# Position-bias rows in two column halves, and two small transposes moved from TensorE to VectorE, in a windowed-attention and expert layer

## The chip, the cores and the metric

The kernel runs on one core of one Trainium2 chip. The metric is the device time in microseconds of one execution; the time given for a kernel is the median of several. TensorE is the matrix engine (PE in the profile; PEld are its weight loads), VectorE is DVE, ScalarE is ACT, GpSimd is POOL, and SyncE (SP) only issues transfers. All data are float32.

## The reference, cut to what matters

The input x is (2, 128, 256, 256): batch, channels, rows, columns. One layer: layer norm over the channels, attention in windows of 8 x 8 pixels with keys from 12 x 12 pixels around them, an output projection and a residual; then, per pixel, a second norm, a router that picks 2 of 8 experts, and their weighted sum as a second residual.

```python
qkv = jnp.einsum('bchw,oc->bohw', x, W_qkv)          # 4 heads of 32
attn = jnp.einsum('bnd,bmd->bnm', q * SCALE, k)
attn = attn + rel_pos_emb(q, rel_height, rel_width) + FIXED_MASK
out = jnp.einsum('bnm,bmd->bnd', jax.nn.softmax(attn, axis=-1), v)
x = x + jnp.einsum('bchw,oc->bohw', out, W_out)
...
router_probs = jax.nn.softmax(t @ router_w + router_b, axis=-1)
top_p, top_i = jax.lax.top_k(router_probs, 2)
```

The mask leaves only keys whose row offset and column offset from the query are both even, so pixels attend only to pixels of their own row parity and column parity. The bias of a query and a key is a product of the query with a row of rel_height (chosen by their difference in rows) plus one with a row of rel_width (difference in columns). After the mask, a window has, for each parity, 4 x 4 queries and 6 x 6 keys, with nine differences in each direction.

## The kernel before, in words

**Tiling.** The image is cut into 64 strips of 8 rows (32 per batch element). A strip has four planes, one per row and column parity, so there are 256 planes of 4 rows x 128 columns = 512 pixels, 32 windows of 16. The channels lie on the 128 partitions. The main loop runs over planes, `n` from 0 to 256 + 6; the last seven rounds only finish experts. Inside `manual_schedule` the order of the instructions on TensorE, VectorE, ScalarE, GpSimd and SP is the order of the calls in the loop.

**One round of the loop**, in the order of TensorE's queue, with the lines of the profile:

- `scores(n)`: the bias is added into the score banks by small matmuls of 32 x 64 array tiles (L447, operand `au`), then queries times keys (L464, `qs`, `kcol`). ScalarE takes the exponential (L472).
- first part of `project(n+1)`: half of the values, `pvv` (L368), copied by ScalarE (L375).
- second part: `pu` (L383), the product of the normed plane `xn` with `wrel`. `wrel` has 128 columns, of which each head uses 18: nine differences of height and nine of width. VectorE turns it in 32 x 32 blocks into `uT` (L385). The call of `states[n + 1]["shift"]()` right after copies from `uT`, with a stride that makes the difference depend on the query's place, into `auT` (L348, two copies), and turns that back into `au` (L353), which the next round's scores read.
- third and fourth part: keys `pk` (L395) and queries `pq` (L417), copied by ScalarE (L406, L413, L419).
- `spread`: the gates `g` (40 columns, four tiles of 128 pixels times 8 experts, a mean and the next layer norm's factor) are turned by TensorE into `pg` (L622), copied by ScalarE to `gT` (L624), stored by SP to `gd` in DRAM (L626), and read back to all partitions: `rb` (L630), `sb` (L659) and `gb` for each expert (L654). 
- four expert products `acc` (L679) of an older row.
- `attend(n)`: row sums (L485), then weights times values (L495); VectorE turns, inverts and multiplies (L505 to L515).
- `norms`: ScalarE squares the rows (L541), TensorE sums them, and makes the router's logits, in 128 x 32 array tiles, `plt` (L547). ScalarE copies them to `lT` (L555), TensorE turns that into `plg` (L558), and VectorE makes mean and deviation from it (`rstd`, L227 to L234, with two ScalarE steps). `route` in the next round (L582 to L615) makes the gates.
- the other half of the values (L368), one product, plg, two products, `out_project` `po` (L523), one product.

VectorE also multiplies the tokens with the gates (`xe`, L670, six of eight experts; GpSimd does two), and adds po and acc to x (L528, L685). GpSimd makes `xn` (L271) and the key columns `xcol` (L330).

**What sets the order.** Every engine works through its own queue in order, and an instruction that waits holds up those behind it. The buffers in PSUM (`ps_mm`) are three, shared by pvv, pu, pk, pq, pg, plt, plg and po. Each DMA in the built program uses one of eight completion semaphores in turn and waits until the DMA before it on that semaphore has landed; before, SP issues all DMAs of the loop. `addr_align` at the head of a round (L786) pads TensorE's program so that each round starts at the same place of a block of 256 instructions.

The softmax here doesn't subtract the row's maximum and nothing guards it: scores larger than these inputs give would overflow.

## Time and profile before

| | us |
|---|---|
| time, median of 3 runs (4543.13 to 4551.57) | 4548.22 |
| the profiled execution: its own time | 4549.69 |
| its span, first to last instruction | 4547.9 |
| TensorE busy | 4490.6 |
| VectorE busy | 3826.1 |
| ScalarE busy | 1582.6 |
| GpSimd busy | 1321.7 |

The profile is one execution. The view of groups gives for each line and engine the number of instructions, their summed time, the mean of one, and how long the engine stood idle just before them and for whom. The chain of waits is followed back from the last instruction: at each step to what released it. Of the span 97% lies on TensorE in that chain. A float32 matmul appears as two MATMUL passes, each with a weight load. Their single durations (595 ns for 512 columns) overlap with the next pass; the chain gives what each adds to the path (430 ns). Groups that the change concerns:

| line | engine, tile | count | mean ns |
|---|---|---|---|
| L383 | PE pu | 512 | 596 |
| L385 | DVE uT | 256 | 717 |
| L348 | DVE auT, 96 elements | 512 | 208 |
| L353 | DVE au | 256 | 1051 |
| L555 | ACT lT | 260 | 266 |
| L558 | PE plg | 260 | 273 |
| L622 | PE pg | 260 | 271 |
| L624 | ACT gT | 260 | 259 |
| L626 | SP gd, 20 KB | 245 | - |

### The profile page before, as it was taken

Reading aid. Unit: us, or ns where it says so; the run is one execution under the profiler, and the core shown is the slowest. Engines: PE = TensorE matmul, PEld = TensorE weight load, DVE = VectorE, ACT = ScalarE, POOL = GpSimd, SP = SyncE. Lnnn points to the kernel's source line nnn. Section 1 sums busy time; section 2 is a strip of 40 time slices with the busy share of each in tenths; the row PEclk is TensorE's granted clock in tenths of the full one; section 3 lists DMA queues with packets and bytes.
Section 4 is the critical chain, followed back from the end, with each engine's and each line's share of the span. In section 5 each row is a group of like instructions: output and inputs, shape, how many; then the busy total and the mean of one; then the engine's idle time right before and its main releaser. Section 6 shows DMA issues by size and latency. Waiting matters only on the chain.

```text
span 4547.9 us, 224166 instructions
## 1 busy us (share of the span) xinstructions
PE 4490.6 (99%) x96841; PEld 2708.2 (60%) x96841; DVE 3826.1 (84%) x11330; ACT 1582.6 (35%) x4542; POOL 1321.7 (29%) x1812
## 2 busy tenths in 40 slices
PE   7999999999999999999999999999999999999997
PEld 5665666565666666666666666666666656656653
DVE  5888888888888888888888888888888888888886
ACT  3333333333333333333333333333333333333331
POOL 1232323232323223232323232323232323232221
PEclk9999999999999999999999999999999999999999
DMA  2565666566556666665656665656666656666655
GB/s 76 176 191 180 190 179 191 181 190 180 189 180 189 183 186 184 186 185 183 188 181 186 183 188 181 190 180 190 180 190 180 191 179 190 182 187 181 188 163 181
DMA packets 457786, 824.84 MB, mean 181 GB/s; under 512 B 52480, under 2 KB 64356, under 8 KB 456804
## 3 DMA queue, kind: packets, MB, share of 16 engines
q1 hardware_dynamic: 456074, 810.21, 59.0%
q8 instruction: 769, 12.60, 1.1%
q14 instruction: 213, 1.74, 0.1%
q10 hardware_dynamic: 730, 0.29, 0.0%
HBM read 737.95 MB, written 72.34 MB: 178 GB/s over the span
## 4 chain that ended last, share of the span: by engine, by line
PE 97%; DVE 1%; issue 1%; DMA 0%; ACT 0%; POOL 0%; SPq 0%; ACTq 0%; DVEq 0%; POOLq 0%
PE acc L679 38%; PE pvv L368 12%; PE att L464 7%; PE att L495 6%; PE plt L547 6%; PE pu L383 5%; PE po L523 5%; PE pk L395 5%; PE pq L417 5%; PE att L447 3%; PE att L485 3%; PE pg L622 1%; PE plg L558 1%; DMA gb<-gd 0%; DVE xe L670 0%
## 5 line engine op out<-in xcount | busy, mean ns | idle before, releaser
L679 PE MATMUL acc<-xe,ew 128*128 128x512 f32 x4096 | 1921.7, 595 | 6.5 <-DVE xt L685 2.6
L679 PEld LDWEIGHTS acc<-xe,ew 128*128 128x128 f32 x4096 | 720.8, 191 | 788.1 <-issue 780.3
L670 DVE TENSOR_TENSOR xe<-xs,gb 128x512 f32<-128x512 f32 x1536 | 950.5, 686 | 10.9 <-DMA gb<-gd 2.2
L674 POOL COPY last<-xe 128x1 f32<-128x1 f32 x256 | 48.3, 189 | 3110.8 <-DVE gb L653 3103.7
L670 POOL TENSOR_TENSOR xe<-xs,gb 128x512 f32<-128x512 f32 x512 | 652.3, 1275 | 5.7 <-PE att L495 2.7
L368 PE MATMUL pvv<-wt,xcol 128*128 128x128 f32 x4096 | 595.1, 288 | 4.2 <-POOL xcol L330 3.1
L368 PEld LDWEIGHTS pvv<-wt,xcol 128*128 128x128 f32 x4096 | 497.2, 191 | 66.6 <-issue 51.9
L555 ACT COPY lT<-plt 128x128 f32<-128x128 f32 x260 | 69.3, 266 | 1141.3 <-PE plt L547 1141.3
L271 POOL TENSOR_TENSOR xn<-xt,rb 128x512 f32<-128x512 f32 x249 | 375.9, 1510 | 79.9 <-DMA rb<-gd 68.1
L464 PE MATMUL att<-qs,kcol 32*64 32x32 f32 x32768 | 391.7, 226 | 2.4 <-issue 2.4
L464 PEld LDWEIGHTS att<-qs,kcol 32*64 32x64 f32 x32768 | 390.3, 130 | 2.6 <-issue 2.6
L375 ACT COPY vv<-pvv 128x512 f32<-128x512 f32 x512 | 300.3, 586 | 207.4 <-PE pvv L368 191.4
L495 PEld LDWEIGHTS att<-pT,vv 64*32 64x32 f32 x32768 | 347.8, 105 | 36.7
L472 ACT ACTIVATE pT<-att 128x1024 f32<-128x1024 f32 x256 | 262.1, 1024 | 253.7 <-PE att L464 250.3
L495 PE MATMUL att<-pT,vv 64*32 64x32 f32 x32768 | 342.5, 200 | 0.0
L385 DVE STREAM_TRANSPOSE uT<-pu 128x512 f32<-128x512 f32 x256 | 183.5, 717 | 150.2 <-PE pu L383 150.2
L541 ACT ACTIVATE sq<-xt 128x512 f32<-128x512 f32 x505 | 292.1, 628 | 0.0
L353 DVE STREAM_TRANSPOSE au<-auT 128x512 f32<-128x512 f32 x256 | 269.2, 1051 | 9.0
L406 ACT COPY kcol<-pk 128x560 f32<-128x560 f32 (+2 forms) x344 | 174.3, 507 | 268.5 <-PE pk L395 265.7
L523 PE MATMUL po<-o,wt 128*128 128x512 f32 x512 | 261.8, 593 | 4.1 <-DVE r__0_619 L227 1.0
L383 PE MATMUL pu<-xn,wrel 128*128 128x512 f32 x512 | 263.6, 596 | 0.0
L417 PE MATMUL pq<-xn,wt 128*128 128x512 f32 x512 | 262.2, 593 | 0.5 <-issue 0.2
(2700 smaller groups left out, 5579.8 us busy)
## 6 DMA issues: line engine op xcount, KB each, us to landing
gb<-gd SPq DMA_DIRECT2D x2048, 256.0 KB
xt<-in_x_dram SPq DMA_DIRECT2D x256, 256.0 KB
sb<-gd SPq DMA_DIRECT2D x256, 256.0 KB
out_dram<-xt SPq DMA_DIRECT2D x256, 256.0 KB
rb<-gd SPq DMA_DIRECT2D x249, 256.0 KB
gd<-gT SPq DMA_DIRECT2D x245, 20.0 KB
ew<-in_L_ffn_expert_w_dram SPq DMA_DIRECT2D x1, 512.0 KB
eb<-in_L_ffn_expert_b_dram SPq DMA_DIRECT2D x1, 512.0 KB
```

What stands on the lines that cost most here:

```text
L271: eng.tensor_tensor(xn[i % 2][:, :, :, k, 1 : PC + 1], ln1_src(i, k).rearrange("p (y j x) -> p y x j", y=2, x=2), rb.rearrange("p (y j x) ...
L368: nc.tensor.matmul(pv[:, t * P : (t + 1) * P], lhsT=xl[:, t0 + t].rearrange("p a k -> p (a k)"), rhs=wv, start=True, stop=True,)
L375: nc.scalar.copy(vv[:, t0 : t0 + 4, :].rearrange("p t c -> p (t c)"), pv)
L383: nc.tensor.matmul(pu, lhsT=wrel, rhs=inner, start=True, stop=True)
L417: nc.tensor.matmul(pq, lhsT=wq, rhs=inner, start=True, stop=True)
L464: nc.tensor.matmul(sc[rows, h, 32 * t : 32 * t + 32], lhsT=kk[hp, half * HP + t, :], rhs=qs[hp, m0 : m0 + 2].rearrange("p m a s -> p (m a ...
L495: nc.tensor.matmul(av[hp, half, 32 * t : 32 * t + 32], lhsT=vv[rows, t, hp], rhs=pT[rows, h, 32 * t : 32 * t + 32], start=True, stop=True,)
L523: nc.tensor.matmul(po, lhsT=wo, rhs=state["o"].rearrange("p f z -> p (f z)"), start=True, stop=True)
L541: nc.scalar.activation(sq, src, AF.Square)
L547: nc.tensor.matmul(plt[32 * t : 32 * t + 32, :P], lhsT=rw[:, j], rhs=src[:, t * P : (t + 1) * P], start=(j == srcs[0][0]), stop=(j == srcs ...
L670: eng.tensor_tensor(self.xe[e], self.xs, self.gb.pop(e), ALU.mult)
L679: nc.tensor.matmul(self.acc, lhsT=ew[:, e, :], rhs=self.xe.pop(e), start=(e == 0), stop=not self.xe)
```

## The change

**Bias.** One of the nine differences of each direction is subtracted from the other eight when `relbd` is built, which adds the same number to all scores of a query and so leaves the softmax as it is. A head then has 16 columns instead of 18, and `wrel` has 64. `pu` becomes two matmuls: the first two rows of the plane into PSUM partitions 0 to 63, the other two into 64 to 127, each 256 columns. `uT` has 256 columns. `shift` makes four copies (two of 96 elements on 64 partitions each, two of 48 on all), two memsets for the difference that is now zero, and a transpose of 256 columns into `both`. A new function `send`, called after the squares of `norms`, moves `both` with eight DMAs on ScalarE's queue, each 16 partitions x 1 KB, to `au`, which is now two fixed buffers that TensorE reads in runs of 8 numbers.

**Statistics and gates.** The copy `lT` goes; VectorE turns `plt` from PSUM straight into `plg` in PSUM in 32 x 32 blocks. `g` is one of three fixed buffers of 2 x 4 x 8 columns; VectorE turns it in SBUF into `gT`, and SP stores it with two DMAs in runs of 128 B. TensorE's `pg` and ScalarE's copy go. `spread` is called before `pu` instead of after `pq`.

```diff
-    relbd = ctile([P, P], "relbd")
+    relbd = ctile([P, HEADS * NB], "relbd")
...
     def shift(uT, n, state):
 
-        for j in range(2):
-            shifted = uT[:, :, :, NU * j + 3 : NU * j + 9]
-            dims = [list(d) for d in shifted.ap]
-            dims[1 + j][0] -= 1
+        to = auT[n % 2]
+        for up, (rows, start) in enumerate(((slice(0, 64), 3), (slice(64, P), 1))):
+            src = uT[rows, :, :, start : start + 6]
+            step, block = src.ap[1][0], src.ap[2][0]
+            dims = [list(src.ap[0]), [step - 1, 2], [block // 2, 8], [1, 6]]
             nc.vector.tensor_copy(
-                auT[n % 2][:, :, :, 6 * j : 6 * j + 6],
-                bass.AP(shifted.tensor, shifted.offset, dims),
+                to[rows, :, :, :, 0:6].rearrange("p a s h k -> p a (s h) k"),
+                bass.AP(src.tensor, src.offset, dims),
             )
-        au = work.tile([P, 2 * NP, PR, 4], F32, tag="au", name=f"au{n}")
-        nc.vector.transpose(au.rearrange("p m a s -> p a s m"), auT[n % 2])
-        state["au"] = au
+        src = uT[:, :, :, NU + 2 : NU + 8]
+        step, block = src.ap[1][0], src.ap[2][0]
+        for h in range(2):
+            dims = [list(src.ap[0]), [step, 2], [block - 1, 4], [1, 6]]
+            nc.vector.tensor_copy(
+                to[:, :, :, h, 6:12], bass.AP(src.tensor, src.offset + h * NB, dims)
+            )
+
+        nc.vector.memset(to[0:64, 0, :, :, 5:6], 0.0)
+        nc.vector.memset(to[:, :, 0, :, 11:12], 0.0)
+        both = work.tile([P, 2 * NP, 8], F32, tag="both", name=f"both{n}")
+        nc.vector.transpose(
+            both.rearrange("p m (a s) -> p a s m", a=2), to.rearrange("p a s h k -> p a s (h k)")
+        )
+        state["both"] = both
+
+    def send(n, state):
+
+        both = state.pop("both")
+        for up in range(2):
+            for h in range(HEADS):
+                r = (up * HEADS + h) * NB
+                nc.scalar.dma_start(au[n % 2][h * DH : h * DH + NB, up], both[r : r + NB])
...
         pu = mm_tile(f"pu{n}")
-        nc.tensor.matmul(pu, lhsT=wrel, rhs=inner, start=True, stop=True)
-        uT = work.tile([P, PR, 4, 32], F32, tag="uT", name=f"uT{n}", bufs=1)
-        nc.vector.transpose(uT, pu.rearrange("p (a m s) -> p a s m", a=PR, s=4))
+        for up in range(2):
+            nc.tensor.matmul(
+                pu[up * 64 : (up + 1) * 64, 0 : NQ // 2],
+                lhsT=wrel,
+                rhs=inner[:, 2 * up : 2 * up + 2],
+                start=True,
+                stop=True,
+            )
+        uT = work.tile([P, 2, 4, 32], F32, tag="uT", name=f"uT{n}", bufs=1)
+        nc.vector.transpose(uT, pu[:, 0 : NQ // 2].rearrange("p (a m s) -> p a s m", a=2, s=4))
...
-        lT = work.tile([P, P], F32, tag="lT", name=f"lT{nm}")
-        nc.scalar.copy(lT, plt[:, :P])
         yield
         plg = mm_tile(f"plg{nm}")
-        nc.tensor.transpose(plg[:, :P], lT, ident)
+        nc.vector.transpose(plg[:, :P], plt[:, :P])
...
-        pg = mm_tile(f"pg{nm}")
-        nc.tensor.transpose(pg[: hi - lo, :P], g[:, lo:hi], ident)
-        gT = small.tile([(E + 2) * NT, P], F32, tag="gT", name=f"gT{nm}")
-        nc.scalar.copy(gT[: hi - lo], pg[: hi - lo, :P])
-        gd = dram.tile([(E + 2) * NT, P], F32, tag="gd", name=f"gd{nm}")
-        nc.sync.dma_start(gd[lo:hi], gT[: hi - lo])
+        gT = small.tile([P, 2, 32], F32, tag="gT", name=f"gT{nm}")
+        nc.vector.transpose(
+            gT.rearrange("p k i -> p (k i)"), g.rearrange("p k b j -> p (k b j)")
+        )
+        gd = dram.tile([2 * E * NT, P], F32, tag="gd", name=f"gd{nm}")
+
+        to = gd.rearrange("(k j t) (b i) -> k (t b) j i", k=2, j=E, i=32)
+        for k in (1, 0):
+            if k or f:
+                nc.sync.dma_start(to[k], gT[:, k])
...
             nxt.fetch(7, nc.scalar)
+            if gated:
+                f, c, made = gated
+                gd, rb1 = spread(f, c, made[0], f"_{n}")
+                row = (*c, rb1) if c else None
+                new = Experts(*f, gd) if f else new
             next(ahead, None)
             if n + 1 < n_planes:
                 states[n + 1]["shift"]()
             next(ahead, None)
             next(ahead, None)
-            if gated:
-                f, c, made = gated
-                gd, rb1 = spread(f, c, made[0], f"_{n}")
-                row = (*c, rb1) if c else None
-                new = Experts(*f, gd) if f else new
...
             next(norm, None)
+            if n + 1 < n_planes:
+                send(n + 1, states[n + 1])
             next(attn, None)
```

More of the change, by code (lines that the diff above doesn't have):

```diff
@@ L1 @@
+import itertools
 from contextlib import ExitStack
@@ L47 @@
 NU = 9
+NB = 16
 @with_exitstack
@@ L187 @@
         for j in range(2):
-            c0 = h * DH + NU * j
-            nc.vector.tensor_copy(
-                relbd[hp, c0 : c0 + NU], relT[j][hp, lo : lo + 2 * NU - 1 : 2]
+            c0 = h * NB + (NU - 1) * j
+            last_d = lo + 2 * (NU - 1)
+            nc.vector.tensor_tensor(
+                relbd[hp, c0 : c0 + NU - 1],
+                relT[j][hp, lo : last_d - 1 : 2],
+                relT[j][hp, last_d : last_d + 1].broadcast_to([DH, NU - 1]),
+                ALU.subtract,
             )
-    wrel = ctile([P, P], "wrel")
+    wrel = ctile([P, HEADS * NB], "wrel")
     pr = mm_tile("p_wrel")
-    nc.tensor.matmul(pr[:, :P], lhsT=wall[:, 0, :], rhs=relbd, start=True, stop=True)
-    nc.vector.tensor_copy(wrel, pr[:, :P])
+    nc.tensor.matmul(
+        pr[:, : HEADS * NB], lhsT=wall[:, 0, :], rhs=relbd, start=True, stop=True
+    )
+    nc.vector.tensor_copy(wrel, pr[:, : HEADS * NB])
     xn, xcol, kcol = [], [], []
@@ L207 @@
         nc.gpsimd.memset(kcol[i][:, NP - 1, KC - 1 : NK : KC], 0.0)
-    auT = []
+    auT, au = [], []
     for i in range(2):
-        auT.append(ctile([P, PR, 4, 32], f"auT{i}"))
+        auT.append(ctile([P, 2, 4, 2, NB], f"auT{i}"))
         nc.gpsimd.memset(auT[i], 0.0)
-        nc.gpsimd.memset(auT[i][:, :, :, KR + 6 : KR + 7], NEG)
+        nc.gpsimd.memset(auT[i][:, :, :, :, KR + 6 : KR + 7], NEG)
+        au.append(ctile([P, 2, 2 * NP, 8], f"au{i}"))
+        nc.gpsimd.memset(au[i], 0.0)
     def rstd(p4, k0, k1, name):
@@ L382, in project @@
         pu = mm_tile(f"pu{n}")
-        nc.tensor.matmul(pu, lhsT=wrel, rhs=inner, start=True, stop=True)
-        uT = work.tile([P, PR, 4, 32], F32, tag="uT", name=f"uT{n}", bufs=1)
-        nc.vector.transpose(uT, pu.rearrange("p (a m s) -> p a s m", a=PR, s=4))
+        for up in range(2):
+            nc.tensor.matmul(
+                pu[up * 64 : (up + 1) * 64, 0 : NQ // 2],
[6 more added lines that the diff above has]
+        nc.vector.transpose(uT, pu[:, 0 : NQ // 2].rearrange("p (a m s) -> p a s m", a=2, s=4))
         state["shift"] = lambda: shift(uT, n, state)
@@ L435, in scores @@
     def scores(n, state):
-        qs, kk, au = state["qs"], state["kk"], state["au"]
+        qs, kk, bias = state["qs"], state["kk"], au[n % 2]
         turn = place(n // 4, 0) // 2
@@ L447, in scores @@
                     nc.tensor.matmul(
-                        sc[rows, h].rearrange("p (t w z) -> p t w z", w=2, z=16)[:, :, w],
+                        sc[rows, h].rearrange("p (t w a z) -> p t w a z", w=2, a=2, z=8)[:, :, w],
                         lhsT=keys[hp, turn, w],
-                        rhs=au[hp, half * NP + w : (half + 1) * NP : 2].rearrange(
-                            "p t a s -> p t (a s)"
+                        rhs=bias[hp, :, half * NP + w : (half + 1) * NP : 2].rearrange(
+                            "p a t z -> p t a z"
                         ),
@@ L529, in out_project @@
         yield
+    gboth = [ctile([P, 2, NT, E], f"g{i}") for i in range(3)]
+    g_turn = itertools.count()
+    for g in gboth:
+        nc.gpsimd.memset(g, 0.0)
     def norms(f, c, nm):
-        g = small.tile([P, (E + 2) * NT], F32, tag="g", name=f"g{nm}")
+        g = gboth[next(g_turn) % len(gboth)]
         srcs = []
@@ L567, in norms @@
             nc.vector.scalar_tensor_tensor(
-                g[:, (E + 1) * NT :], u[:, 1 - k0], 3.0, r[:, 1 - k0], ALU.add, ALU.mult
+                g[:, 1, :, 1], u[:, 1 - k0], 3.0, r[:, 1 - k0], ALU.add, ALU.mult
             )
@@ L590, in route @@
         nc.vector.tensor_tensor(
-            g[:, E * NT : (E + 1) * NT].unsqueeze(2), sd, p4[:, :, E : E + 1], ALU.subtract
+            g[:, 1, :, 0:1], sd, p4[:, :, E : E + 1], ALU.subtract
         )
@@ L613, in route @@
         nc.vector.tensor_tensor(sm, sm, rs, ALU.mult)
-        g1 = g[:, 0 : NT * E].rearrange("p (e t) -> p t e", t=NT)
-        nc.vector.tensor_tensor(g1, gate, sm.broadcast_to(by_e), ALU.mult)
+        nc.vector.tensor_tensor(g[:, 0], gate, sm.broadcast_to(by_e), ALU.mult)
         yield
     def spread(f, c, g, nm):
-        lo, hi = (0 if f else (E + 1) * NT), ((E + 2) * NT if c else (E + 1) * NT)
-        pg = mm_tile(f"pg{nm}")
-        nc.tensor.transpose(pg[: hi - lo, :P], g[:, lo:hi], ident)
-        gT = small.tile([(E + 2) * NT, P], F32, tag="gT", name=f"gT{nm}")
-        nc.scalar.copy(gT[: hi - lo], pg[: hi - lo, :P])
-        gd = dram.tile([(E + 2) * NT, P], F32, tag="gd", name=f"gd{nm}")
-        nc.sync.dma_start(gd[lo:hi], gT[: hi - lo])
+        gT = small.tile([P, 2, 32], F32, tag="gT", name=f"gT{nm}")
+        nc.vector.transpose(
+            gT.rearrange("p k i -> p (k i)"), g.rearrange("p k b j -> p (k b j)")
+        )
+        gd = dram.tile([2 * E * NT, P], F32, tag="gd", name=f"gd{nm}")
[3 more added lines that the diff above has]
+                nc.sync.dma_start(to[k], gT[:, k])
         rb = None
@@ L745 @@
     states[0]["shift"]()
+    send(0, states[0])
     if n_planes > 1:
```

## The prediction

> **What bounds the kernel now.** I read the page's first part, then the chain of waits over one plane, then who waited for whom, then the timeline of that plane. The page:

> ```profile
> PE 4490.6 (99%) x96841; PEld 2708.2 (60%) x96841; DVE 3826.1 (84%) x11330; ACT 1582.6 (35%) x4542; POOL 1321.7 (29%) x1812
> ```

> TensorE is busy 99% of the span. A busy TensorE may still hide waits, so the chain must say whether anything else is in it. Columns: start us, length us, engine, tile and line:

> ```profile
> 2013.07 0.60 PE att L447 x30
> 2013.67 1.34 PE att L464 x80
> 2015.01 1.09 PE pvv L368 x8
> 2016.10 0.86 PE pu L383 x2
> 2016.96 0.86 PE pk L395 x2
> 2017.82 0.86 PE pq L417 x2
> 2018.68 0.11 PE pg L622
> 2018.79 3.44 PE acc L679 x8
> 2022.22 0.57 PE att L485 x14
> ...
> 2023.95 1.01 PE plt L547 x32
> ...
> 2026.91 0.11 PE plg L558
> ```

> The next plane's L447 starts at 2030.45, so a plane is 17.38 us, and only TensorE stands in it: what is taken off TensorE comes off the end, as long as nobody else is late. The three pieces the change touches are pu 0.86, pg 0.11 and plg 0.11 us. VectorE is the nearest rival for the bound:

> ```profile
> DVE uT L385 <- PE pu L383: 150.2, 253, 4.5
> DVE xt L528 <- PE po L523: 47.8, 145, 0.8
> ...
> PE pg L622 <- DVE g L615: 17.5, 6, 3.5
> ```

> The first two say that VectorE waits for TensorE in most planes; the longest wait the other way round is the third, six times in all, near the two ends. In the stretch from 2000 to 2500 us VectorE is busy 425.38 of 500 us, 14.8 us per plane. In each plane it waits for TensorE about 1.4 us: uT 0.59, xt 0.19, sT and xt after acc 0.11, and 0.5 at L227 for plg (0.51 in the plane above). The remaining 17.38 - 14.8 - 1.4 = 1.2 us are gaps between its own instructions and trips to ScalarE.

> [...]

> ```profile
> 2024.12 0.40 PE L547 MATMUL plt<-sq,rw 128*32 128x128 f32 x8
> 2024.34 0.40 PE L547 MATMUL plt<-xt,rw 128*32 128x128 f32 x8
> ```

> Eight passes over 128 columns start per 0.22 us, where one alone (pg, plg) takes 0.11: four at a time. Two groups of 64 columns over all 128 rows appear nowhere in this trace. [...] Going in, L485 has two rounds of 256 columns (0.43, since 512 columns are 0.43 per pass) and takes 0.57; L447 has four rounds of 128 (0.43) and takes 0.60: 0.14 to 0.17 above the streams. Going out, pvv after L464 or L547 takes 1.09 for eight passes of 0.11 (0.89): 0.20 above. [...] the new gd stores have runs of 128 B, and no run here shows such a store.

> **The change part by part** (per plane, 256 planes; times from the profiled execution).

> 1. *pg and plg leave TensorE*: 0.11 + 0.11 = 0.22 us, all on the path, in about 254 planes: -55 us.

> 2. *pu*: two passes of 512 columns (0.86) become four of 256, two at a time: 0.43. But pvv before and pk after are full-array work, so the pair pays one switch in (0.14 to 0.17) and one out (0.20), which pu did not. I take 0.43 + 0.15 + 0.19 = 0.77: the single records give 0.093 drain each way, 0.05 for the first 64-column load, 0.10 for the first 128-column load of pk. Saved 0.09, x256 = -23 us. Ends: 0.06 to 0.13. The halving is mostly eaten by the two switches.

> 3. *L447's operand* now comes as runs of 8 floats instead of 16, with the same 128 columns. No pass here reads runs of 8; reads of 16 and of 512 go at one rate (0.107 per 128). I take 0; the bad end is a doubled pass, +0.43.

> 4. *TensorE's program*: 378 loads, 378 matmuls, 3 waits and 9 fillers of 0.07 us fill 768 places per plane. After: 378, 378, 6 and 6; planes with two pk parts 380, 380, 7 and 1. It still fits. The waits and fillers run some 3 us ahead of the array (the fillers end 3 us before L447 starts): 0.

> 5. *VectorE*. Taking two-size pairs of rows (L596: 256 elements 425 ns; L670: 512 elements 686) gives 164 ns + 1.02 per element. Scaled so, uT goes from 717 to 440, the bias transpose from 1051 to 610, plg (128 columns) is 300, gT (64) 230. The shift has two copies of 96 elements (208 each, as L348) and two of 48 (160) for two of 208: +320; two memsets at 59: +120. Sum: -280 - 440 + 300 + 230 + 320 + 120 = +0.25 us. Ends: about 0, if plg and gT cost little more than the fixed 164, and +1.25 if the transposes do not shrink and the extra semaphores of the last one (four at 0.07) are paid. Its own need is 14.8 + 1.2 + 0.25 = 16.25 against TensorE's new 17.38 - 0.31 = 17.07: hidden, 0 us. That cover is 0.8 us; beyond it every further 0.1 us costs 26 us. The g-chain moves before uT, but VectorE waited there for pu 0.54 us anyway (idle before uT at 2017.00).

> 6. *ScalarE*: the lT and gT copies go (266 + 259 ns). Eight DMA issues come in after the squares. SP's issues take 0.29 to 0.32, ScalarE's own few at the start 0.46 to 0.54: 2.3 to 4.3 us in its queue. Behind them stand the xt copy and the vv copy, and po waits for the latter (its PSUM buffer). The place is idle now:

> ```profile
> 2025.03 0.27 ACT L555 COPY lT<-plt 128x128 f32<-128x128 f32 x1 [4.22 <-PE plt L547]
> ```

> The gap of 4.22 us holds nearly all of that, and po starts 1.9 us after the vv copy ends: 0. If the sends took over 6 us, po would be late and each 0.1 us would cost 26.

> 7. *The bias now arrives by DMA.* The issues start at 2020.8, after the squares, and end at 2023.1 to 2025.1; the bias is needed at 2030.1. A small gd store let rb start 1.3 us after its own issue; 256 KB loads land in 3.3 to 4.9. So it is there between 2024.4 and 2030.0: hidden, by 5.7 us or, at the far end, by next to nothing; I take a landing of 3.3, 3.7 us of cover. Without cover each 0.1 us costs 26.

> 8. *SP's queue*: gd goes out 3 us earlier, so rb is early. Each DMA waits for the one eight before it, and the sends now count among them: sb, gb0 to gb2 and the x load wait for sends and start about 1.5 us later. Their first user (xs, next plane) comes 14 us after. The new traffic is 128 packets of 1 KB and 256 of 128 B per plane; at the page's mean of 94 ns a packet (59.0% of 16 engines for 456074 packets) that is at most 2.3 us on engines that are busy 60% of 17.4: 0.

> 9. *The ends.* At the start the first scores follow the shift by 3 us only; the sends and a landing add about 4.5, and planes 1 to 4, which have no expert products to hide them, about 0.8 each: +8 (3 to 15). In the last seven rounds the products no longer stand behind pg, which waited for route (the 17.5 us above): next late is VectorE itself, 12 instead of 13 us a round: -6 (0 to -20).

> Sum: -55 - 23 + 8 - 6 = -76. The profiled execution took 4549.69 us (its span 4547.9 and 1.8 around it): 4474. The median of three is 1.5 below it: **4472 us**, 1.7% faster. The likeliest case's own range is 4450 to 4495.

> **Rivals.** *The halves do not run at once* (the slower end): four passes of 0.213 and the switches are 1.19 instead of 0.86, +0.33 x 256 = +85; with -55 and +2: 4580. It decides once the pair streams for more than 0.73 us. Against it: L547 runs four at a time over all rows. For it: both halves share one stationary and only two groups of 64 columns were never seen. *Partly at once*, that is, the second pass of the first half blocks the second half: three rounds, 0.98, +31: 4526; this is also the case that the change does not do what it says. *VectorE takes over*: at the far end of step 5 it needs 17.25 a plane instead of 17.07: +46, 4518. For it: it has the most added instructions; against it: the two transposes it halves cost 1.77 us today. *ScalarE or the arrival of the bias*: 0.3 us late per plane is +77, 4549; against it the covers of steps 6 and 7.

> **How the numbers follow.** Likeliest 0.74; halves in series 0.06; partly at once 0.04; VectorE 0.09; ScalarE, arrival or the 8-float read 0.07 (4500 to 4600). About 0.2% (9 us) is what a measurement of this kernel can tell from no change. Faster: 0.74 + 0.04 + 0.07 of VectorE's + 0.01 of the last = 0.86; same 0.04; slower 0.10 (the series and most of the last). A range of 4445 to 4530 takes the likeliest case, the partial one and most of VectorE's, and leaves out about 0.15.

> **What would show it.** In the chain after: no pg or plg; pu at 0.7 to 0.8 us with pk's first pass late by 0.1; 17.07 us from L447 to L447; VectorE still waiting for TensorE. Wrong if L447's successor waits for a DMA, if po waits for ScalarE, if pu's four passes start one after the other, or if VectorE's waits for TensorE are gone.

## The result, and the profile after

The changed kernel takes 4770.67 us (median of 4 runs, 4766.52 to 4783.51) against 4546.16 for the kernel before (4 runs): a ratio of 1.050, 95% interval 1.047 to 1.052. It is 5% slower where 1.7% faster was forecast. The profiled execution took 4766.52 us, its span is 4764.7, and the granted clock is much the same in both kernels (0.995, and 0.997 before).

Three lines of the page: busy time by engine, the queue that brings in the program, and the group of the key products `pk` (busy, mean ns | idle time just before):

```profile
PE 4516.4 (95%) x96833; PEld 2692.2 (57%) x96833; DVE 3807.7 (80%) x12874; ACT 1493.3 (31%) x4022; POOL 1322.1 (28%) x1817
...
q8 instruction: 769, 12.60, 1.0%
...
L437 PE MATMUL pk<-xn,wt 128*128 128x512 f32 (+2 forms) x528 | 357.4, 685 | 185.9 <-issue 185.2
```

The same group in the kernel before:

```profile
L395 PE MATMUL pk<-xn,wt 128*128 128x512 f32 (+2 forms) x528 | 261.0, 578 | 0.0
```

TensorE has fallen from 99% to 95% busy: it now waits. VectorE has fallen too, from 84% to 80%, so it is not the new bound. And `pk`, which the change doesn't touch, now has idle time in front of it, with the releaser "issue", which stands for a wait that the profile can't tie to any engine or transfer. The view of waits (us in total, times, longest) says the same:

```profile
ACT xt L118 <- DMA au<-both: 1084.7, 246, 6.3
...
PEld pk L437 <- issue: 320.0, 268, 2.2
...
DVE sT L547 <- PE att L537: 311.9, 253, 3.2
...
PE pk L437 <- issue: 185.2, 237, 1.7
```

The largest of these is harmless: ScalarE waits 4.4 us per plane (1084.7 over 246) until earlier sends of its own have landed and free a completion semaphore (a lane, below), and nothing that TensorE takes from it next is late. VectorE still waits for TensorE. What is left is `pk`. The chain of waits reaches back only over the last microseconds in this run, so I read one plane in the timeline instead (start, length, engine, operation; in brackets the idle time before):

```profile
2017.13 0.65 PE L419 MATMUL pu<-xn,wrel 128*64 128x256 f32 x4
...
2017.71 0.70 PE L437 MATMUL pk<-xn,wt 128*128 128x512 f32 x1
...
2019.52 0.19 PEld L437 LDWEIGHTS pk<-xn,wt 128*128 128x128 f32 x1 [1.62 <-issue]
2019.52 0.70 PE L437 MATMUL pk<-xn,wt 128*128 128x512 f32 x1 [1.11 <-issue]
...
2020.06 1.02 PE L459 MATMUL pq<-xn,wt 128*128 128x512 f32 x2
```

The two passes of one and the same float32 product start 1.81 us apart; in the kernel before they start 0.43 apart. Nothing that the second pass reads is missing, since the first pass read the same tiles. So I took every plane's starts from the trace's records and averaged each phase over 248 planes, those of rounds 7 to 254, in which no phase is missing (ns from a phase's first start to the next phase's; some short phases are left out; e1 to e10 are experiments below):

| phase | before | after | e1 | e6 | e8 | e10 |
|---|---|---|---|---|---|---|
| bias and scores (L447 before, L489 after) | 1944 | 1956 | 1952 | 1953 | 1943 | 1950 |
| first half of pvv | 995 | 1088 | 1088 | 1088 | 995 | 1088 |
| pu | 864 | 583 | 583 | 583 | 864 | 583 |
| pk | 853 | **1977** | 963 | 960 | 853 | 960 |
| pq | 866 | 861 | 931 | 861 | 861 | 861 |
| pg | 124 | - | - | - | - | - |
| four products | 3542 | 3524 | 3553 | 3524 | 3524 | 3524 |
| weights times values (L495, L537) | 1286 | 1397 | 1381 | 1400 | 1268 | 1287 |
| plg and three products | 2689 | 2577 | 2579 | 2577 | 2577 | 2577 |
| a plane | 17425 | 18230 | 17294 | 17210 | 17159 | 17092 |

The parts that the change meant to shrink did shrink. The plane is longer because `pk` takes 1.0 us more than it does in e1, and the weights times values 0.11 more than before.

**Where the 1.0 us is.** TensorE's program comes in by packets of its own: 769 on queue q8, 12.60 MB, that is 16.4 KB each, three per plane. The trace of after has 96833 loads, 96833 matmuls, 1549 waits and 1740 fillers in that program, 256 for each packet, and that is the kernel's `BLOCK`. So I take a packet for one block. `addr_align` with `FIRST_LIMIT` 95 makes a block end behind the 95th instruction of a round, so the next ones end behind the 351st and the 607th. I count a load and a matmul for each pass, and the waits:

- before: 64 (L447) + 256 (L464) + 17 (pvv and a wait) + 4 (pu) + 4 (pk) + 4 (pq) + 2 (pg) = 351. The block ends exactly behind pg, ahead of the products.
- after: 64 (L489) + 4 (waits for the sends' DMAs, new) + 256 + 17 + 8 (pu in halves) + 2 (first pass of pk) = 351. The block ends exactly between the two passes of pk.

In the changed kernel the packet of the next block ends 3.72 us after the round's first pass starts, and pk's second pass starts 1.37 us after that (medians; 90% of the latter lie between 1.24 and 1.53): at about 5.1 us. From round to round the packet's end moves by over a microsecond, and the pass moves with it (correlation 0.96). In the kernel before TensorE got to its block end after 1.944 + 0.995 + 0.864 + 0.853 + 0.866 + 0.124 = 5.65 us, so the block was there (its packet ends 3.83 us into the round, median). In the changed kernel it gets there after 1.956 + 1.088 + 0.583 + 0.43 = 4.06 us. That is a theory from a count and from times that go together; e1, e2 and e3 move the block's end and nothing else.

### The profile page after: what moved, and what is told of

The parts are those of the page before. It is cut to its first block, busy times and chain, and to the rows that moved or that the text cites. A ratio compares the mean times of both kernels' runs of the same rounds, so it can differ in the third digit from the quotient of the medians.

```text
span 4764.7 us, 228335 instructions
## 1 busy us (share of the span) xinstructions
PE 4516.4 (95%) x96833; PEld 2692.2 (57%) x96833; DVE 3807.7 (80%) x12874; ACT 1493.3 (31%) x4022; POOL 1322.1 (28%) x1817
## 3 DMA queue, kind: packets, MB, share of 16 engines
q8 instruction: 769, 12.60, 1.0%
## 5 line engine op out<-in xcount | busy, mean ns | idle before, releaser
L727 PE MATMUL acc<-xe,ew 128*128 128x512 f32 x4096 | 1887.3, 594 | 20.1 <-DVE gb L701 19.3
L727 PEld LDWEIGHTS acc<-xe,ew 128*128 128x128 f32 x4096 | 759.0, 190 | 885.1 <-issue 862.0
L437 PE MATMUL pk<-xn,wt 128*128 128x512 f32 (+2 forms) x528 | 357.4, 685 | 185.9 <-issue 185.2
L547 DVE STREAM_TRANSPOSE sT<-att 128x512 f32<-128x512 f32 x256 | 183.5, 717 | 311.9 <-PE att L537 311.9
L537 PEld LDWEIGHTS att<-pT,vv 64*32 64x32 f32 x32768 | 372.5, 105 | 47.0 <-issue 2.1
L118 ACT COPY xt<-onesm 128x1 f32<-128x1 f32 x247 | 47.3, 192 | 1090.6 <-DMA au<-both 1084.7
L537 PE MATMUL att<-pT,vv 64*32 64x32 f32 x32768 | 375.8, 200 | 1.9 <-issue 1.9
L437 PEld LDWEIGHTS pk<-xn,wt 128*128 128x128 f32 x528 | 98.5, 189 | 415.6 <-issue 320.0
L570 DVE TENSOR_TENSOR xt<-po,xt 128x512 f32<-128x512 f32 x256 | 177.1, 692 | 145.2 <-PE po L565 145.2
```

Source lines behind the costliest of these rows:

```text
L437: nc.tensor.matmul(pk[:, : m * PC], lhsT=wk, rhs=xp[:, part[0] : part[0] + m, 1 : PC + 1], start=True, stop=True,)
L537: nc.tensor.matmul(av[hp, half, 32 * t : 32 * t + 32], lhsT=vv[rows, t, hp], rhs=pT[rows, h, 32 * t : 32 * t + 32], start=True, stop=True,)
L547: nc.vector.transpose(sT, av[:, 2:4])
L727: nc.tensor.matmul(self.acc, lhsT=ew[:, e, :], rhs=self.xe.pop(e), start=(e == 0), stop=not self.xe)
```

## The experiments

**e1: the changed kernel, block end six places later.**

```diff
-BLOCK, FIRST_LIMIT = 256, 95
+BLOCK, FIRST_LIMIT = 256, 101
```

> The changed kernel with only FIRST_LIMIT raised from 95 to 101, so that the second block of 256 instructions of TensorE's program ends behind pq, as it does in the kernel before (behind pg), and not between pk's two passes. Theory (program fetch): the second pass of pk waited 1.01 us a plane for its block; with the boundary behind pq the array has 1.4 us more work queued when the program runs dry. The stall goes, wholly or nearly: 4770 - 250 = about 4510, and 4480 if the 0.11 us in L537 goes with it; faster than the kernel before by 0.8 to 1.5%. Rival (the two halves themselves, or the change of the array's tiling, hold up the pass behind them): the wait stays where pk's second pass is, 4770. Rival (VectorE, ScalarE or the transfers are late behind the stall): the stall goes but another wait takes its place, 4550 to 4770.

Measured 4531.3 us against 4543.35 (ratio 0.997, 0.996 to 0.998): 239 us less than the change as it stood. The block then ends behind pq, right ahead of the products, as it did behind pg in the kernel before. It falls some 21 us short of the 4510 expected: in the mean pq still takes 0.07 us and the four products 0.03 us longer than in e6, whose block ends later (table).

**e2: the kernel before, block end between pk's passes.**

```diff
-BLOCK, FIRST_LIMIT = 256, 95
+BLOCK, FIRST_LIMIT = 256, 87
```

> The kernel before with only FIRST_LIMIT lowered from 95 to 87, so that its block boundary falls between the two passes of pk, where the changed kernel has it. Theory (program fetch): pk's second pass waits about 0.95 us a plane, as it would be reached 4.2 us after the start of L447 and its block is there at 5.2: 4546 + 240 = about 4790, slower by 5%. Rival (halves or tiling): nothing moves, 4546.

Measured 4765.78 us (ratio 1.049, 1.047 to 1.051). One number in the kernel before gives a loss of 222 us, as large as that of the change, without any of it.

**e3: the changed kernel, block end in front of pk.**

```diff
-BLOCK, FIRST_LIMIT = 256, 95
+BLOCK, FIRST_LIMIT = 256, 93
```

> The changed kernel with FIRST_LIMIT 93: the boundary falls before pk's first pass, with 0.53 us less work queued than at 95. Theory (program fetch): the block comes at the same time, so both passes of pk run after it and the stall grows by 0.5 us a plane: 4770 + 130 = about 4900. Rival (halves or tiling): 4770.

Measured 4891.81 us (ratio 1.077, 1.075 to 1.078). The wait grows from 1.01 to 1.42 us per plane, by about the one pass (0.43) that no longer lies ahead of the end: the block comes at the same time (3.63 + 1.42 = 5.05 us into the round, against 4.06 + 1.01 = 5.07 in after), and there is less work to hide it.

The groups of pk in e1 and in e2, and e3's view of waits:

```profile
L437 PE MATMUL pk<-xn,wt 128*128 128x512 f32 (+2 forms) x528 | 289.4, 632 | 0.0
```

```profile
L395 PE MATMUL pk<-xn,wt 128*128 128x512 f32 (+2 forms) x528 | 327.8, 629 | 154.1 <-issue 150.1
```

```profile
PEld pk L437 <- DVE auT L376: 239.6, 119, 2.6
...
PE pk L437 <- DVE auT L376: 188.2, 121, 2.1
```

In e1 pk waits for nothing; in e2 it waits in the old kernel. The third fence is a warning: in e3 the same wait is put down to VectorE's memset in auT (L376), which pk doesn't read. A releaser is inferred, and here the inferred one merely happened to end then. "issue" in front of an instruction whose sibling with the same operands has just run is the truer sign.

**e4 and e8: the second part of the change alone** (VectorE turns plg and gT, `spread` ahead of pu; bias rows as before).

```diff
-BLOCK, FIRST_LIMIT = 256, 95
+BLOCK, FIRST_LIMIT = 256, 93
...
-        lT = work.tile([P, P], F32, tag="lT", name=f"lT{nm}")
-        nc.scalar.copy(lT, plt[:, :P])
         yield
         plg = mm_tile(f"plg{nm}")
-        nc.tensor.transpose(plg[:, :P], lT, ident)
+        nc.vector.transpose(plg[:, :P], plt[:, :P])
...
```

> The kernel before with the second part of the change alone: plg and gT are turned by VectorE, spread stands before pu; pu, uT, shift and au stay as before. FIRST_LIMIT 93 keeps the block boundary behind pq. Theory: 0.22 us a plane leaves TensorE and nothing takes its place: 4546 - 55 - 6 at the end = about 4485. Rival (VectorE's two transposes, 0.57 us, or the 128-byte stores of gd are on the path): 4546 or slower.

Measured 4493.3 us (ratio 0.989, 0.987 to 0.990). In e8 the limit is 109, so that the block ends behind the fourth product:

> The turns alone (second part of the change), with FIRST_LIMIT 109 instead of 93, that is, the boundary behind the four expert products. At 93 pq waited 0.04 us a plane. Theory (program fetch): 4493 - 10 = about 4483. Rival: 4493.

Measured 4481.77 us (ratio 0.985, 0.984 to 0.987). Its page:

```profile
PE 4425.1 (99%) x96321; PEld 2686.2 (60%) x96321; DVE 3997.4 (89%) x11850; ACT 1468.9 (33%) x4022; POOL 1317.9 (29%) x1815
```

TensorE is back at 99% and VectorE, with 89%, still not the bound.

**e9: the same shift without the change**, so that e8 isn't credited with what the place of the block gives.

```diff
-BLOCK, FIRST_LIMIT = 256, 95
+BLOCK, FIRST_LIMIT = 256, 111
```

> The kernel before, with FIRST_LIMIT 111 in place of 95: the second block of TensorE's program then ends behind the fourth expert product instead of in front of the first. Control for the turns alone at 109, which were 66 us under the kernel before. Theory (the turns themselves bring most of that): here only the small remains of the wait for the program go, 0.02 us at pg and 0.02 at the products per plane, 4536 to 4541. Rival (most of the 66 us came from the place of the block's end): 4500 or less.

Measured 4540.83 us (ratio 0.9987, 0.9981 to 0.9994). The kernel before was losing some 6 us at its block end already (its mean pg falls from 124 to 109 ns in e9, its four products from 3542 to 3528); the rest of e8's gain is the turns'.

**e6: the changed kernel, block end behind the fourth product.**

```diff
-BLOCK, FIRST_LIMIT = 256, 95
+BLOCK, FIRST_LIMIT = 256, 117
```

> The changed kernel with FIRST_LIMIT 117: the boundary lies behind the four expert products, so the array has 3.4 us more work queued than at 101. At 101 pq still waited 0.09 us a plane and the products 0.03 in the mean. Theory (program fetch): these go, 4531 - 22 = about 4509. Rival (the rest of the loss is elsewhere): 4531.

Measured 4516.24 us (ratio 0.992, 0.991 to 0.994). No phase waits for the program now, and yet the whole change is 34 us behind its second part alone, where the forecast had it 23 us ahead. What is left stands in the table: the weights times values, 1400 ns against 1268. In the records of that phase some of its 128 short passes follow the pass before them over 0.08 us later than in e8's median round: 148 such pauses in e6, none in the kernel before. All 148 end within 0.45 us after the end of an issue of one of ScalarE's sends, most of them 0.39 to 0.41 us after it.

**e5 and e7: the eight sends on SP.** The first idea was that ScalarE's queue was at fault. e5 has e1's block end.

```diff
-BLOCK, FIRST_LIMIT = 256, 95
+BLOCK, FIRST_LIMIT = 256, 101
...
-                nc.scalar.dma_start(au[n % 2][h * DH : h * DH + NB, up], both[r : r + NB])
+                nc.sync.dma_start(au[n % 2][h * DH : h * DH + NB, up], both[r : r + NB])
```

> The changed kernel with the boundary behind pq (FIRST_LIMIT 101) and the eight sends of the bias issued by SP instead of ScalarE. In the run with the boundary moved alone (4531), L537 still took 0.11 us a plane more than before; its pauses of 0.1 to 0.2 us begin within 0.3 us after the end of a ScalarE DMA issue. Theory (an issue on ScalarE's queue holds up TensorE's stream of narrow passes): the pauses go, 4531 - 28 = about 4503. Rival (the transfers themselves or the new layout slow L537): 4531. Rival (SP's queue, now 22 issues a plane, delivers the gates late): above 4531.

Measured 5131.11 us (ratio 1.128, 1.126 to 1.129): the expectation fell, by over 600 us. The timeline of one plane (SPq is SP's queue of DMA issues):

```profile
2007.95 1.43 SPq L674 DMA_DIRECT2D gd<-gT  x2
...
2009.79 3.70 PE L727 MATMUL acc<-xe,ew 128*128 128x512 f32 x8 [0.86 <-issue]
...
2012.67 0.33 SPq L678 DMA_DIRECT2D rb<-gd  x1
2013.10 5.42 SPq L389 DMA_DIRECT2D au<-both  x8
```

SP's issues come in order. The load of rb, which waits for gd's stores, goes out at 2012.67, the sends behind it from 2013.10, and the loads of gates behind them from 2019.24: all come in bunches, and the packet of the program, 0.98 us long and so hardly longer than before (0.95 in after), starts 4.9 us into the round instead of 2.8 and ends at 5.9 instead of 3.7. Now TensorE waits at the products, and they start 1.42 us after the packet's end (median of the 244 rounds in which they wait). What delays it is not shown. The pauses in the weights times values were there as well, 298 of them, nearly all ending 0.38 to 0.40 us after the end of an issue of a send, now SP's. So they go with the sends and not with ScalarE. e7 moves that block end as in e6:

> Both of the above: sends on SP, and FIRST_LIMIT 117. If the two causes are apart, their gains add: 4531 - 28 - 22 = about 4480, some 10 us below the run with the turns alone (4493). If not, 4500.

Measured 5117.39 us (ratio 1.125, 1.124 to 1.127). This fell too: the wait moved to the next block end, inside L537, which takes 2.88 us there. With the transfers bunched the placement of one end doesn't help. The loss in these two need not all be waiting for the program: the granted clock was 0.977 in e5 and 0.960 in e7, against 0.994 in e1. In 52 of e5's 248 rounds and 89 of e7's the trace shows half the clock for some 3.5 to 4 us, and these rounds are 2.6 and 3.0 us longer than the others, 134 and 264 us in all. Which comes first, the wait or the lower clock, isn't shown.

**e10: half of the sends on GpSimd**, with e6's limit, so that nearly all are issued before the short passes begin.

```diff
-                nc.scalar.dma_start(au[n % 2][h * DH : h * DH + NB, up], both[r : r + NB])
+                queue = (nc.scalar, nc.gpsimd)[up]
+                queue.dma_start(au[n % 2][h * DH : h * DH + NB, up], both[r : r + NB])
```

> The changed kernel with FIRST_LIMIT 117 (4516 us), and four of the eight sends (the second half of the bias) issued by GpSimd instead of ScalarE. ScalarE's issues then end some 2.4 us earlier, ahead of the weights times values (L537). Theory (the narrow passes of L537 pause at ScalarE's issues): L537 falls from 1.41 to about 1.29 us per plane, and the time by 30 us to 4486. Rival one (the pauses come with the sends' data or with an issue on any queue): L537 stays at 1.4 and the time at 4516. Rival two (GpSimd, waiting for the transposed rows, holds up its own products and xn): over 4530.

Measured 4472.14 us (ratio 0.983, 0.982 to 0.985). Timelines of a plane in e6 and in e10, the sends and the weights times values:

```profile
2003.12 5.43 ACTq L389 DMA_DIRECT2D au<-both  x6
...
2005.46 1.49 PE L537 MATMUL att<-pT,vv 64*32 64x32 f32 x128
```

```profile
2010.14 2.08 POOL L390 DMA_DIRECT2D au<-both  x4 [7.50 <-DVE both L378]
...
2011.91 1.24 ACTq L390 DMA_DIRECT2D au<-both  x2
...
2013.36 1.34 PE L538 MATMUL att<-pT,vv 64*32 64x32 f32 x128
```

In e6 ScalarE is still issuing while the short passes run, and they take 1.49 us; in e10 both queues are done before, and they take 1.34. Counted over the 248 planes (issues that end in the phase or up to 0.25 us ahead of it):

| | before | e6 | e10 | e8 |
|---|---|---|---|---|
| issues of sends, 16 KB | 0 | 342 | 130 | 0 |
| SP's issues, loads of 256 KB | 335 | 491 | 390 | 256 |
| pauses over 80 ns in the phase | 0 | 148 | 12 | 0 |
| the phase, ns | 1286 | 1400 | 1287 | 1268 |

The issues of SP's loads of 256 KB go without pauses; those of the sends go with them. (Of the 1286 ns before, the 18 above e8's lie behind the last short pass, where the next phase starts late.) The trace of e10 also tells an issue from the data that it moves. In 120 of its 248 rounds no issue of a send ends in the phase or up to 0.3 us ahead of it, while 36 of the sends' 1 KB packets in the mean start in it: there the short passes are as fast as in e8, within 1 ns. So the pauses go with the issuing and not with the data on its way. GpSimd is busier (41% instead of 29%), and TensorE waits for it 1.5 us in all. The first seven rounds, which e6 took 119.4 us for, take 105.4; of the 44 us between e6 and e10, 14 lie there and 28 in the weights times values.

## Why the prediction was wrong, step by step

The step that failed is the fourth, *TensorE's program*: "It still fits. The waits and fillers run some 3 us ahead of the array (the fillers end 3 us before L447 starts): 0." It counted how many places a plane fills (768, three blocks) and not where in the plane a block ends. Both halves of the change moved that: pu in halves has four instructions more, the sends bring four waits ahead of the scores, and pg's two ahead of the end are gone. The end slid from "behind pg" into pk, and the work ahead of it shrank from 5.65 to 4.06 us while the block still came at 5.1. Cost: 1.977 - 0.963 (e1) = 1.014 us x 248 planes = 251 us, where the step had 0. Shown by e1 (taken away), e2 (made in the old kernel) and e3 (made larger by one pass).

The difference between the spans of after and e10 is 4764.7 - 4470.4 = 294 us: (1.977 - 0.960) x 248 = 252 at pk, (1.397 - 1.287) x 248 = 27 in the weights times values, 13 in the first seven rounds (118.4 against 105.4), and 2 elsewhere.

The other steps, measured:

- Step 1, *pg and plg leave TensorE*, -55: held. The plg phase lost 0.112 us, and pg's was 0.124 long, with 0.016 that it waited (its median is 0.108). e8 is some 60 us under e9 (ratios 0.9852 and 0.9987), both with their block end behind the fourth product.
- Step 2, *pu*, -23: held. The two halves run at once: pu fell from 864 to 583 ns. Of that pvv's end and pk's start give back 93 and 110 ns, so that the pair with its two switches takes 93 + 583 + 110 = 786 ns where the step had 0.77 us. pvv, pu and pk together: 2712 before, 1088 + 583 + 963 = 2634 in e1, 0.078 us or 20 us in all.
- Step 3, *L447's operand in runs of 8*: held. The phase's median is 1944 ns in e9 and in e6; its mean is 12 ns longer in after, 3 us in all, from single planes.
- Step 5, *VectorE*: held, with less to spare than forecast. The groups of its parts add up to +0.40 us per plane instead of +0.25 (in after uT takes 450 ns, `both` 644, plg 326, gT 245, the copies 209 and 187, the memsets 62 and 65), within the step's ends. TensorE isn't held up by it in the main loop, but in e10 uT waits for pu in 11 rounds only, against 253 in the kernel before.
- Step 6, *ScalarE*: the cost was mis-sized, 5.4 to 7.4 us of queue per plane (after and e1) instead of 2.3 to 4.3, since an issue takes 0.51 to 0.60 us and the later ones wait for a lane, one of the eight completion semaphores (in after each has 705 DMAs, and a send lands 3.8 us after its issue starts, median). In the main loop it stayed hidden all the same, also where it took over the 6 us at which the step had po late (in the first rounds of after po waits for ScalarE once, 3.8 us). But what the step didn't think of is that an issue goes with pauses on another engine: 27 us, the second largest loss. e10 shows that it depends on when the sends are issued.
- Step 7, *The arrival of the bias*: held in the main loop: the scores' phase has a median of 1946 ns in after against 1944 before, and a mean of 1956 against 1944. In the first seven rounds it didn't hold: there L489 waits 4.2 us in all for these DMAs, in 11 waits.
- Step 8, *SP's queue*: held as built. e5 shows how little was to spare: eight issues more in that queue cost 600 us over e1, part of it at a lower clock. gd's stores in runs of 128 B landed in 2.7 to 3.0 us (medians in e4, e8 and e10).
- Step 9, *The ends*, +8 and -6: in after +2 until the first scores and +19 in the first seven rounds, more than the 3 to 15 of the step; -4 at the tail. In e10 +2, +6 and -3.

With the fourth step and the sends mended, e10 is at 4472.14 us, where the sum stood at 4472. That they agree so closely is luck: the plane is 17092 ns where 17070 was forecast, which is 5 us too long in all, and e10's later block end also saves the 6 us or so that e9 saves, which no step had. Still, with both losses out of the way the other terms of the sum came out near their sizes, and none of the rivals came true: the halves were not in series, VectorE didn't take over, and in the main loop nothing came late by DMA except the program itself, which no rival named.

Whether the halves are worth having beside the turns is less sure: e10 and e8 stand at 0.9835 (0.982 to 0.985) and 0.9852 (0.984 to 0.987), and their intervals overlap. The spans say 14 us: 0.067 us x 248 = 17 less in the planes, some 3 more at the ends.

## What to carry to other kernels

When TensorE is full and its program is long, count its instructions to the next block end, waits included, and ask how much array time lies ahead of that end: a change that removes work and adds instructions can slide the end to a place where the block isn't there yet. Re-tune the alignment with each such change (one number was worth 239 to 254 us here, more than the change itself), and put the end behind a row of long passes (in e6 it lies behind 3.5 us of products, and no phase waits for it). If a pass waits for "issue" and its sibling with the same operands has just run, look at the program's own packets first; and see which short passes run while small transfers are issued.
